# Seven quarter products for eight in the weighting of the values: an attention and cluster-MLP kernel on one core

## The chip, the cores and the metric

The kernel runs on one core of a Trainium2 chip, as one launch. The metric is the device time of that launch in microseconds (us), the median of several runs. The engines that a core has are called as in the profile: PE (TensorE; PEld is its loading of weights), DVE (VectorE), ACT (ScalarE), POOL (GpSimd) and SP (SyncE, which here only starts DMAs). They run side by side, each takes its own instructions strictly in the order of the program, and semaphores tie them together.

## What is computed

The input is four images of 256 channels and 64 x 64 pixels, f32 throughout. Two layers follow each other. The first is self-attention over the N = 4096 pixels of an image:

```python
q = jnp.einsum('oc,bcn->bno', wq, xf) + bq           # 32 channels
k = jnp.einsum('oc,bcn->bon', wk, xf) + bk[None, :, None]
attn = jax.nn.softmax(jnp.einsum('bnd,bdm->bnm', q, k), axis=-1)
v = jnp.einsum('oc,bcn->bon', wv, xf) + bv[None, :, None]
out = jnp.einsum('bcn,bmn->bcm', v, attn).reshape(B, Cc, H, W)
return gamma[0] * out + x
```

The second is a block with a clustering of the pixels and an MLP, each behind a group norm and with a residual:

```python
y = x + ls1 * cluster(group_norm(x, ...), f_w, f_b, v_w, v_b, proj_w, proj_b, alpha, beta)
hdn = conv1x1(jax.nn.gelu(conv1x1(group_norm(y, ...), mlp_w1, mlp_b1)), mlp_w2, mlp_b2)
y = y + ls2 * hdn
z = relu(batch_norm(y * dw_w, ...))
z = relu(batch_norm(conv1x1(z, pw_w), ...))
```

The change is in the product of v with the exponentials, the last einsum of the attention; the weights of the MLP and of the cluster are only stored elsewhere.

## The kernel before

**Stages.** The images are worked on one after the other. For each there are three stages: `weighting` (the attention), `cluster`, and `mlp`, which also computes the first scores of the next image. `alone` makes what the first image needs before its weighting. The program is written under `tc.manual_schedule()`: each engine executes what concerns it in the order in which the Python code issues it, and that order, made by hand, is all the schedule there is.

**Units and blocks.** The scores of an image are a 4096 x 4096 matrix. It is cut into `NBLK` = 8 blocks of 512 queries, a block into `GRP` = 8 units (steps) of 512 keys, so an image has 64 units. A unit's tile `s` in SBUF is 128 keys x 4 quarters x 512 queries. It goes through these functions:

- `score(u)` (L316): four products of 32 rows into two PSUM tiles of the pool `ps_s`, which has two such tiles. ACT copies both to `s` (L351, L356), DVE folds both into the running maximum `top` (L355, L358; L353 in the first unit of a block). Scores are made `LEAD` = 9 units ahead, by `due(u, quarter)`, which looks into the table `at`; in most units this happens ahead of the unit's first quarter.
- `across` and `spread`: the maximum over the keys is turned by PE (L369), reduced by DVE (L371), put on a diagonal (L373) and spread over all partitions by a product with ones (L383); the result `mb` stays in PSUM, in a tile of the pool `ps_m`, which has two. `across` runs ahead of the last quarter of unit 6 of the block before, `spread` right after the score of unit 7.
- `exps(u)`: DVE subtracts `mb` from each half of `s` (L395), ACT takes the exponential (L398), both in place; POOL adds the halves to the sum `acc` (L400, L403). It is issued one unit ahead.
- `weigh(u, av, quarter)` (L408): for each of four quarters, two products of 128 x 128 values with 512 columns of `s` are added to the two accumulators `av` in PSUM, one for each half of the channels. The accumulators have one buffer each, so the next block's first products wait until they are read.
- at the end of a block `gather` adds the two halves of `acc` (POOL, L420) and `clear` takes `av` out of PSUM, times gamma, one half by ACT (L424) and one by DVE (L425). During the next block follow `total` (L429), `inverse` (L435), `add` (POOL: times the inverse, L439, and onto the image, L444), `seen` and `pooled` (statistics, L448 and L453).

Each f32 product of PE appears as two MATMUL and two LDWEIGHTS instructions in the profile.

**Weights.** `w1_s`, `w2_s` and `mix` (the weights of the cluster's projections with room for 32 more columns) are loaded or made once at the start and stay. In `derived`, POOL turns two quarters of `w1_s` into the sums that the MLP needs, because `mlp` itself makes its hidden layer with seven quarter products of 256 columns in place of eight (L1126).

**What hides what.** `fill` takes products of the next image (or, in the last image, those of a block of the image before, `late_block`) and puts them where the chain of the group norm and the cluster leaves PE idle.

## Time and profile before

| what | value |
|---|---|
| median of three runs | 3478.5 us (3478.35 to 3481.72) |
| the profiled execution | 3478.09 us, of which its span 3476.0 us |
| mean granted clock of TensorE | 0.997 |
| PE busy | 3421.1 us, 98% of the span |
| DVE busy | 2046.2 us, 59% |
| ACT busy | 1683.9 us, 48% |
| POOL busy | 1489.2 us, 43% |

The span is the time from the first to the last instruction of one execution. Busy times count instructions under way, so an engine at 98% can still have a slower or a faster way to do the same. Of the groups of instructions (line, engine, operation, tile written <- tiles read, shape, count | busy us, mean ns | idle us before, and what ended it), these belong to the work around the change:

```profile
L408 PE MATMUL av<-s,v 128*128 128x512 f32 x4096 | 1826.5, 597 | 0.6 <-ACT s L398 0.6
L403 POOL TENSOR_TENSOR acc<-acc,s 128x1024 f32<-128x1024 f32 x448 | 1057.5, 2361 | 466.1 <-ACT s L398 446.7
L398 ACT ACTIVATE s<-s 128x1024 f32<-128x1024 f32 x512 | 538.7, 1057 | 462.8 <-DVE s L395 429.4
L395 DVE TENSOR_TENSOR s<-s,mb 128x1024 f32<-128x1024 f32 x512 | 595.2, 1207 | 6.5 <-PE mb L383 6.5
L355 DVE TENSOR_TENSOR top<-sc,top 128x1024 f32<-128x1024 f32 x196 | 239.9, 1224 | 388.0 <-PE sc L333 388.0
L333 PE MATMUL sc<-q,k 32*128 32x512 f32 x2048 | 294.0, 640 | 1.4 <-DMA q<-q 1.4
```

[...]

### The profile page before, as it was taken

Reading aid. Unit: us, or ns where it says so; the run is one execution under the profiler, and the core shown is the slowest. Engines: PE = TensorE matmul, PEld = TensorE weight load, DVE = VectorE, ACT = ScalarE, POOL = GpSimd, SP = SyncE. Lnnn points to the kernel's source line nnn. Section 1 sums busy time; section 2 is a strip of 40 time slices with the busy share of each in tenths; the row PEclk is TensorE's granted clock in tenths of the full one; section 3 lists DMA queues with packets and bytes.
Section 4 is the critical chain, followed back from the end, with each engine's and each line's share of the span. In section 5 each row is a group of like instructions: output and inputs, shape, how many; then the busy total and the mean of one; then the engine's idle time right before and its main releaser. Section 6 shows DMA issues by size and latency. Waiting matters only on the chain.

```text
span 3476.0 us, 31760 instructions
## 1 busy us (share of the span) xinstructions
PE 3421.1 (98%) x11760; PEld 1694.3 (49%) x11760; DVE 2046.2 (59%) x2912; ACT 1683.9 (48%) x2157; POOL 1489.2 (43%) x799
## 2 busy tenths in 40 slices
PE   8999999999999999999999999999999999999999
PEld 4444445655444444565544444466554444445565
DVE  4666664645566666464556666646446666664543
ACT  5545553444554554344455555434445554544444
POOL 2656665211265665521126566552104665672200
PEclk9999999999999999999999999999999999999999
DMA  2000001000000000100000000000000000000000
GB/s 91 7 4 3 7 0 49 7 19 13 20 5 4 3 7 12 37 7 19 19 16 4 3 5 5 19 30 7 19 19 10 4 7 3 4 0 1 13 19 25
DMA packets 25260, 47.16 MB, mean 14 GB/s; under 512 B 6704, under 2 KB 8592, under 8 KB 25104
## 3 DMA queue, kind: packets, MB, share of 16 engines
q1 hardware_dynamic: 20240, 38.29, 3.2%
q10 hardware_dynamic: 4608, 6.30, 0.8%
q8 instruction: 93, 1.52, 0.2%
q0 software_dynamic: 256, 0.52, 0.1%
q14 instruction: 63, 0.52, 0.0%
HBM read 19.93 MB, written 16.78 MB: 11 GB/s over the span
## 4 chain that ended last, share of the span: by engine, by line
PE 94%; DVE 3%; ACT 1%; DMA 0%; issue 0%; SPq 0%; POOL 0%; ACTq 0%; DVEq 0%
PE av L408 52%; PE mo L1133 12%; PE sc L333 8%; PE hu L1126 4%; PE pw L1102 3%; PE hp L1126 3%; PE hq L1126 3%; PE vp L285 2%; PE fv L790 2%; PE mb L383 1%; PE den L429 1%; PE op L911 1%; PE qp L304 0%; PE kp L262 0%; PE tt L369 0%
## 5 line engine op out<-in xcount | busy, mean ns | idle before, releaser
L408 PE MATMUL av<-s,v 128*128 128x512 f32 x4096 | 1826.5, 597 | 0.6 <-ACT s L398 0.6
L408 PEld LDWEIGHTS av<-s,v 128*128 128x128 f32 x4096 | 758.9, 190 | 1024.6 <-issue 1015.1
L403 POOL TENSOR_TENSOR acc<-acc,s 128x1024 f32<-128x1024 f32 x448 | 1057.5, 2361 | 466.1 <-ACT s L398 446.7
L398 ACT ACTIVATE s<-s 128x1024 f32<-128x1024 f32 x512 | 538.7, 1057 | 462.8 <-DVE s L395 429.4
L395 DVE TENSOR_TENSOR s<-s,mb 128x1024 f32<-128x1024 f32 x512 | 595.2, 1207 | 6.5 <-PE mb L383 6.5
L1133 PE MATMUL mo<-hs,w_s 128*128 128x512 f32 x992 | 508.4, 596 | 3.8 <-ACT hs L1155 1.6
L355 DVE TENSOR_TENSOR top<-sc,top 128x1024 f32<-128x1024 f32 x196 | 239.9, 1224 | 388.0 <-PE sc L333 388.0
L1155 ACT ACTIVATE hs<-hs,pv_s 128x256 f32<-128x256 f32 x496 | 251.3, 508 | 360.9 <-DVE hs L1162 350.1
L351 ACT COPY s<-sc 128x1024 f32<-128x1024 f32 x224 | 226.1, 1009 | 350.9 <-PE sc L333 350.9
L1162 DVE TENSOR_TENSOR hs<-hu,hs 128x256 f32<-128x256 f32 x372 | 157.8, 424 | 355.0 <-ACT hs L1165 205.5
L1088 POOL TENSOR_TENSOR xn<-xn 128x256 f32<-128x256 f32 x27 | 23.8, 881 | 681.7 <-DVE xn L1075 433.4
L333 PE MATMUL sc<-q,k 32*128 32x512 f32 x2048 | 294.0, 640 | 1.4 <-DMA q<-q 1.4
L400 POOL TENSOR_TENSOR acc<-s 128x1024 f32<-128x1024 f32 x32 | 75.1, 2347 | 476.9 <-ACT s L398 476.9
L358 DVE TENSOR_TENSOR top<-sc,top 128x1024 f32<-128x1024 f32 x196 | 240.1, 1225 | 47.5 <-ACT s L351 30.9
L356 ACT COPY s<-sc 128x1024 f32<-128x1024 f32 x224 | 226.9, 1013 | 76.0 <-DVE top L355 39.8
L1162 DVE TENSOR_TENSOR hs<-hq,hs 128x256 f32<-128x256 f32 x372 | 146.4, 421 | 107.5 <-PE hq L1126 103.3
L1133 PEld LDWEIGHTS mo<-hs,w_s 128*128 128x128 f32 x992 | 186.9, 190 | 42.7 <-ACT hs L1165 7.3
L333 PEld LDWEIGHTS sc<-q,k 32*128 32x128 f32 x2048 | 81.0, 182 | 192.5 <-issue 106.6
L1126 PE MATMUL hp<-xn,w_s 128*128 128x256 f32 x496 | 150.6, 385 | 2.7 <-DVE xn L1075 2.7
L1126 PEld LDWEIGHTS hp<-xn,w_s 128*128 128x128 f32 x496 | 92.4, 190 | 73.0 <-issue 62.4
L285 PE MATMUL vp<-wv_s,x 128*128 128x256 f32 x512 | 123.4, 387 | 0.2 <-ACT v L293 0.2
L1102 PE MATMUL pw<-xn,wpw_s 128*128 128x512 f32 x248 | 112.0, 594 | 3.4 <-ACT xn L1196 2.2
(215 smaller groups left out, 2823.0 us busy)
## 6 DMA issues: line engine op xcount, KB each, us to landing
x<-in_x SPq DMA_DIRECT2D x32, 512.0 KB, 4.6
out<-xn SPq DMA_DIRECT2D x62, 256.0 KB, 2.1
q<-q ACTq DMA_DIRECT2D x96, 64.0 KB, 2.0
w_s<-in_w SPq DMA_DIRECT2D x2, 1024.0 KB, 8.9
q<-q SPq DMA_DIRECT2D x24, 64.0 KB, 2.0
q<-q POOLq DMA_DIRECT2D x8, 64.0 KB, 6.4
out<-xl SPq DMA_DIRECT2D x2, 256.0 KB, 2.0
wv_s<-in_wv SPq DMA_DIRECT2D x1, 256.0 KB, 7.1
```

The source lines that it names most:

```text
L333: nc.tensor.matmul(halves[r // 2][:, r % 2, :], k_s[rows, g, :], q_s[rows, :], start=True, stop=True)
L355: nc.vector.tensor_tensor(top, halves[1], top, ALU.max)
L356: nc.scalar.copy(s[:, 2:4, :], halves[1])
L358: nc.vector.tensor_tensor(top, halves[0], top, ALU.max)
L395: nc.vector.tensor_tensor(sh, sh, mxs[nb].unsqueeze(1).to_broadcast([P, 2, NB]), ALU.subtract)
L398: nc.scalar.activation(sh, sh, AF.Exp)
L403: nc.gpsimd.tensor_tensor(acc, acc, s[:, 2 * h : 2 * h + 2], ALU.add)
L408: nc.tensor.matmul(av[c], own["v"][:, RG * g + quarter, c * P : (c + 1) * P], slots[u][:, quarter, :], start=(g == 0 and quarter == 0), st ...
L1126: nc.tensor.matmul(out, w[:, j * P : (j + 1) * P], x, start=True, stop=True)
L1133: yield nc.tensor.matmul(acc[c], w2_s[:, jj, c * P : (c + 1) * P], hs[:, i], start=(j == 0 and i == 0), stop=(j == HID // P // 2 - 1 and i ...
L1155: nc.scalar.activation(dst, src, act, bias=bias)
L1162: nc.vector.tensor_tensor(dst, ps, term, ALU.add)
```

## The change

In the units 2 to 6 of each block but an image's first (`SEVEN`), the product of v with the exponentials is no longer made quarter by quarter. A pair of the unit's value quarters gives a 2 x 2 matrix of blocks A (two row blocks: 128 channels each; two column blocks: 128 keys each), and the exponentials give B (two rows: the same keys; two columns: 256 queries each). Seven products of sums of these blocks replace the eight of blocks (Winograd's form). Each is issued for two pairs (i = 0, 1), with 256 columns.

- The sums of v are made once an image, in its first block, by DVE (`value_sums`), in place or in the memory of the MLP's weights, which are not needed then.
- The sums of the exponentials are made in each unit: two by DVE one unit ahead (`ready`), two by POOL in the unit itself, behind the product that still reads the old value (`by_seven`). The last two products read what POOL makes.
- Three of the products go to accumulators of their own (`pms`, both tiles of `ps_m`), and `combined` adds these up at unit 7, into `t`; `clear` then adds `av` to `t`, both halves by DVE.
- The sum `acc` over the keys, for the softmax, is taken from the sums made, where there are some.
- As `ps_m` is taken, the turned and the spread maximum use a tile of `ps_s`, and ACT copies the spread one to SBUF (`dg`), from where DVE's subtraction reads it.
- `spread` and the `exps` behind it are issued after the second quarter of unit 7; the score of unit 7 ahead of its last quarter, that of unit 0 ahead of its third, that of unit 1 ahead of its second.
- `add` is cut into two halves, at units 3 and 5; statistics come later.
- v is scaled by gamma when it is taken out of PSUM, so `clear` doesn't.
- `w1`, `w2` and `mix` are loaded for each image at the end of its weighting, and POOL's two sums of w1 made then.

The diff, cut:

```diff
+    own_w = {}
+    def load_mix(b):
+        own_w["mix"] = swap.tile([P, KC, 2, 2 * ED + 32], F32, tag="mix", name=f"mix_{b}")
+        for f in range(2):
+            nc.sync.dma_start(
+                out=own_w["mix"][:, :, f, 16 : 16 + 2 * ED],
+                in_=wfv.rearrange("(k p) m -> p k m", p=P),
+            )
...
+    def load_mlp(b):
+        w1_s = own_w["w1"] = swap.tile([P, KC, HID], F32, tag="w1", name=f"w1_{b}")
+        w2_s = own_w["w2"] = swap.tile([P, HID // P, C], F32, tag="w2", name=f"w2_{b}")
+        nc.sync.dma_start(out=w1_s, in_=w1.rearrange("(k p) m -> p k m", p=P))
+        nc.sync.dma_start(out=w2_s, in_=w2.rearrange("(k p) m -> p k m", p=P))
...
+        nc.gpsimd.tensor_tensor(w_cd, w_cd, w_d, ALU.add)
+        nc.gpsimd.tensor_scalar(w_d, w_d, -1.0, None, ALU.mult)
...
         def spread(nb, dg):
+            dg = dg.rearrange("p j n -> p (j n)")
+            if nb:
+                mb = ps_s.tile([P, 2, NB], F32, tag="s", name=f"mb_{b}_{nb}")[:, 0]
+            else:
+                mb = ps_m.tile([P, NB], F32, tag="m", name=f"mb_{b}_{nb}")
+            nc.tensor.matmul(mb, ones, dg, start=True, stop=True)
+            if nb:
+                nc.scalar.copy(dg, mb)
+            mxs[nb] = dg if nb else mb
...
+        def plain(u):
...
+            if g == 0:
+                nc.gpsimd.tensor_tensor(acc[:, 0], s[:, 0], s[:, 1], ALU.add)
+            for r in range(2 if g == 0 else 0, RG):
+                nc.gpsimd.tensor_tensor(acc[:, 0], acc[:, 0], s[:, r], ALU.add)
...
+        def ready(u):
+            b11, b12, b21, b22 = pairs(u)
+            nc.vector.tensor_tensor(u3_of(u), b12, b22, ALU.add)
+            nc.vector.tensor_tensor(b12, b12, b11, ALU.subtract)
...
+            product(av[0], 0, a12, b21)
+            product(pm[0], 0, a11, b11, start=one)
+            nc.gpsimd.tensor_tensor(b11, b11, u3, ALU.subtract)
+            nc.gpsimd.tensor_tensor(b21, b21, b11, ALU.add)
+            product(av[0], 1, w3, b22)
+            product(pm[1], 0, w7, u3, start=one)
+            product(pm[1], 1, s1, b12, stop=end)
+            acc = accs[nb][:, 1].rearrange("p (x n) -> p x n", x=2)
+            for x, t in enumerate((u3, b21)):
+                if one:
+                    nc.gpsimd.tensor_tensor(acc[:, x], t[:, 0], t[:, 1], ALU.add)
+                else:
+                    for i in range(2):
+                        nc.gpsimd.tensor_tensor(acc[:, x], acc[:, x], t[:, i], ALU.add)
+            between()
+            product(pm[0], 1, s2, b11, stop=end)
+            product(av[1], 0, a22, b21)
...
+            nc.scalar.copy(c11, p1)
+            nc.vector.tensor_tensor(c21, p6, c11, ALU.add)
+            nc.vector.tensor_tensor(c12, p5, c21, ALU.add)
+            nc.vector.tensor_tensor(c21, p7, c21, ALU.add)
+            nc.vector.tensor_tensor(c22, p5, c21, ALU.add)
...
         def clear(nb, av):
...
+            for c in range(KC):
+                nc.vector.tensor_tensor(ts[nb][:, c], av[c], ts[nb][:, c], ALU.add)
...
-        at = {(u, 0): u + LEAD for u in range(units - LEAD)}
+        place = {7: 3, 0: 2, 1: 1}
+        at = {(u, place.get(u % GRP, 0)): u + LEAD for u in range(units - LEAD)}
...
+                if u == units - 1:
+                    load_mix(b)
+                    load_mlp(b)
...
+                if seven(u):
+                    by_seven(u, av, beside)
+                    turn()
+                else:
                     weigh(u, av, 0)
                     due(u, 1)
                     weigh(u, av, 1)
+                    if g == GRP - 1 and more:
+                        spread(nb + 1, own["dg"])
+                        exps(u + 1)
+                        plain(u + 1)
+                    if nb and g == 0:
+                        total(nb - 1)
+                    due(u, 2)
+                    beside()
+                    weigh(u, av, 2)
+                    turn()
+                    due(u, 3)
+                    weigh(u, av, 3)
```

`beside` issues, for the unit ahead, `ready` or `plain`, and for the block before its inverse, its halves of `add` and its statistics. `turn` is `across` in unit 6.

## The prediction

> **What bounds the kernel now.** I read the page's chain of waits first, then the chain in one block of the attention, then the busy time of each engine over four such blocks, and last the timelines of DVE and POOL where they meet. The page's chain:

> ```profile
> PE 94%; DVE 3%; ACT 1%; DMA 0%; issue 0%; SPq 0%; POOL 0%; ACTq 0%; DVEq 0%
> PE av L408 52%; PE mo L1133 12%; PE sc L333 8%; PE hu L1126 4%; PE pw L1102 3%; PE hp L1126 3%; PE hq L1126 3%; PE vp L285 2%; PE fv L790 2%; PE mb L383 1%; PE den L429 1%; PE op L911 1%; PE qp L304 0%; PE kp L262 0%; PE tt L369 0%
> ```

> TensorE sets the end, and over half of that is the weighting of the values (L408). The chain inside a block has no hole:

> ```profile
> 1040.60 5.35 PE av L408 x12
> 1045.95 0.44 PE tt L369 x4
> 1046.39 1.72 PE av L408 x4
> 1048.11 1.07 PE sc L333 x8
> 1049.18 1.05 PE mb L383 x2
> 1050.23 6.87 PE av L408 x16
> 1057.10 1.07 PE sc L333 x8
> 1058.17 3.63 PE av L408 x8
> 1061.80 0.86 PE den L429 x2
> ```

> A logical f32 product is two instructions here: 8 of them are "x16" in 6.87 us, 0.429 us an instruction of 512 columns. With the changes of shape around the score (0.1 us each) a step is 7.07 + 1.07 us. A block of eight steps takes 67.1 us (69.1 with the next queries, L304), and the other engines have this to do in it:

> ```profile
> core 0: us, PE busy (x) PEld busy (x) DVE busy (x) ACT busy (x) POOL busy (x), PEclk, DMA share, GB/s
> 1049.18:1118.27 69.09, 69.09 (x217) 27.73 (x217) 44.75 (x42) 35.18 (x36) 41.63 (x18) 1.00 0.02 5
> 1118.27:1185.40 67.13, 67.13 (x200) 27.23 (x200) 44.76 (x42) 35.13 (x35) 41.64 (x18) 1.00 0.02 4
> ```

> DVE 44.8 and POOL 41.6 of 67.1 us: a third is free on each, if they can run side by side. The next lines are where they do not. DVE's fold (L363) reads two tiles of SBUF, POOL's L420 too:

> ```profile
> 1043.54 1.59 POOL L420 TENSOR_TENSOR rden<-acc 128x512 f32<-128x512 f32 x1
> ...
> 1043.29 0.72 DVE L363 TENSOR_TENSOR top<-top 128x512 f32<-128x512 f32 x1
> ...
> 975.10 1.28 POOL L420 TENSOR_TENSOR rden<-acc 128x512 f32<-128x512 f32 x1
> ...
> 976.05 0.89 DVE L363 TENSOR_TENSOR top<-top 128x512 f32<-128x512 f32 x1
> ```

> Where POOL came 0.25 us after the fold, it took 1.59 us instead of 1.26 to 1.28: it waited 0.31 of the 0.47 us that the fold still had. Where the fold came while POOL had 0.33 us left, it took 0.89 instead of 0.69. So one waits for the other's end less 0.14 us. Against DVE's L395 (one input in PSUM) POOL's L403 keeps its 2.36 us, and L395 its 1.21.

> [...]

> **The change, part by part.**

> *Products.* A changed step has 7 products of 2 pairs at 256 columns: 28 instructions in place of 16 of 512. Consecutive instructions of L1126 (256 columns) start 0.216 us apart, so 28 x 0.216 = 6.05 us for 6.87: 0.82 us gained. Steps: 5 x 7 blocks (not the first) x 4 images = 140, so **-115 us** if nothing waits. A changed step is then 6.05 + 1.07 + about 0.1 = 7.2 us, a block 63.1. The weight load is 0.19 us, under 0.216, as in L1126.

> *Block boundary.* The maximum's spread (L383) went from the start of step 7 to behind its second quarter, and the score of step 7 from the start to before its last quarter. DVE now clears both halves of av (before: ACT and DVE one each). What is queued ahead of that clearing, counted from the start of step 7: products to 3.43, mb to 4.29, then in turn ACT's copy of mb 0.6, DVE's two subtractions 2 x 1.21, the second exp 1.06, ACT's copy of the score (in ACT's queue behind that exp) 1.01, DVE's maximum of the score (L353) 1.22, the first clear 0.69, some 0.1 for each of seven hand-overs: 4.29 + 7.0 + 0.7 = 12.0 us. TensorE is done with the step at 3.43 + 0.86 + 1.72 + 1.07 + 1.72 = 8.8 and needs the cleared accumulator for its next product. It waits 3.1 us where before it had none. Six boundaries of an image have such a score (the seventh has no later unit): 24 x 3.1 = **+74 us**.

> *POOL and DVE.* Subtractions: mb is copied to SBUF, so 16 of them a block now have two SBUF inputs. "ready" adds 10 DVE instructions of 512 elements (0.685 each, L346), all from SBUF. POOL: in a changed step two of 512 (L936, L1059: 1.27) and four of 256 (L1090: 0.724; two in the first); 5.4 us where L403 took 4.72. add: four of 512, 5.1 us in steps 3 and 5. The new wait is TensorE's own: the last two products read b11 and b21, which POOL makes in the same step after product 2. Without a clash they come in time: 2.6 us of POOL against products 3 to 5 and 6, 3.46 us.
> Now the stretch from POOL's first b11 (step 2) to its last b21 (step 6). POOL: 5 x 2.54 + 14 x 0.724 + 5.1 = 27.9 us. DVE in that time: 8 subtractions 9.7, 8 "ready" 5.5. They exclude each other; take 16 x 2 x 0.14 = 4.5 off for hand-overs, add 1.1 for POOL's gaps of 0.075 between its own. 27.9 + 15.2 - 4.5 + 1.1 = 39.7 us. TensorE would be there after 4 x 7.2 + 3.46 = 32.3. It waits 7.4 us a block. Last block of an image: no scores, 28.1 us of TensorE, so 11.6. 24 x 7.4 + 4 x 11.6 = **+224 us**. The bounds: over a whole block the sum of both engines is 46.8 + 27.6 (with fold and dg) - 7.8 + 1.3 = 67.9 us against 63.1, so 4.8 a block or 135 us if every lag could be worked off in steps 7, 0 and 1; and 0 if the clashes fell into POOL's idle time. Above: DVE has 54 us of work in a block and strict order; its waits delay its maxima, which hold the two score buffers, so up to 10 a block, 280 us. I take the middle sum, as the wait is within a step and can't be worked off later.

> *Rest.* Sums of the values (20 DVE instructions of 256 in the first block, 8 us an image): DVE has 20 us idle there, 0. "combined", 4 x 0.42 and one ACT copy at the start of step 7: before the spread, 0 (1.7 a block if DVE is late, within the bound above). v scaled on ACT at 0.69 for 0.585: ACT is half idle, 0. tt and mb in the score's buffers: free in those quarters, 0. At an image's end the clear goes ahead of the reciprocal: 2 x 0.69, **+5 us** for four. The weights: SP gets four DMAs at the last step, behind the x loads; nothing but outputs stands behind them. W1 landed in 8.9 us at the start; POOL's two of 1.27 wait for it, with "begin" behind them. Only in the last image is W1 read at once, by the fill after the last step: 0 to 8, taken as **+3**. The start drops 2 MB behind the x loads: 0.

> Sum: -115 + 74 + 224 + 5 + 3 = +191 on 3478 (the profiled execution: span 3476.0, 3478.1 with 2.1 around it; the median of the runs, 3478.5, is the same): **3670 us**.

> **Rivals.**
> 1. Faster: DVE's clashes fall into POOL's 37% idle time, so that TensorE never waits for b11 or b21. For: POOL needs only 5.4 of 7.2 us, and TensorE's wait at the boundary lets both catch up. Against: 67.9 us of both in 63.1. Time: 3478 - 115 + 74 + 8 = 3445. It decides where clashes cost POOL under 1.3 us a changed step (7.2 less 5.4 of work and 0.45 of gaps), of the 3.8 us that DVE's four instructions hold. With the boundary hidden too, by work that I put in the wrong order, 3371.
> 2. Lags are worked off in the plain steps, only the sum binds: 4.8 us a block, of which the boundary's 3.1 is a part: 3478 - 115 + 135 + 8 = 3506.
> 3. Likeliest, both waits stand: 3670, its own range 3550 (5 a block with the boundary half hidden) to 3740 (10 a block).

> **Chances.** Likeliest 0.70, rival 2 0.10, rival 1 0.15 and 0.05 with the boundary hidden. A measurement of this kernel tells about 0.2% (7 us) from no change. Faster 0.18, within 0.2% 0.04 (between rivals 1 and 2), slower 0.78. The range 3435 to 3740 leaves out half of the faster cases below and the worst stalls above.

> **What will show it.** Right: DVE's L395 line well over 1.21 us in mean (1.6 or more); POOL's 512-element additions over 1.27; the chain of waits going through POOL and DVE, over 5%; TensorE waiting for POOL at the last two products, and for DVE at each block's first product; blocks of 70 to 76 us. Wrong: blocks near 63 us, L395 at 1.2, or POOL idle before each b11 for want of TensorE's product 2.

## The result, and the profile after

The kernel with the change takes 3827.6 us (median of four runs, 3826.2 to 3829.0), the kernel before, on the same chip, 3478.9: a ratio of 1.100 with the interval [1.0981, 1.1019], 349 us more. The forecast was 3670 us. Its sign holds, its size doesn't: the time lies above the range (3435 to 3740).

The page of the kernel after; first the two lines of its chain of waits, then groups (busy us, mean ns of one, idle us before and what ended it):

```profile
PE 49%; DVE 32%; POOL 7%; ACT 6%; issue 6%; DMA 0%; SPq 0%; POOLq 0%; ACTq 0%; DVEq 0%
DVE s L417 13%; PE av L545 11%; PE mo L1305 11%; DVE top L374 5%; PE hu L1298 4%; ACT s L367 4%; DVE s L486 3%; PE pw L1274 3%; PE hp L1298 3%; PE hq L1298 3%; PE vp L299 3%; DVE u L485 2%; PE sc L349 2%; DVE rden L585 2%; PE av L503 2%
...
L545 PE MATMUL av<-s,v 128*128 128x512 f32 x1856 | 895.9, 631 | 107.3 <-DVE t L575 84.2
...
L417 DVE TENSOR_TENSOR s<-s,dg 128x1024 f32<-128x1024 f32 x448 | 678.6, 1554 | 28.4 <-ACT dg L409 28.0
...
L439 POOL TENSOR_TENSOR acc<-acc,s 128x512 f32<-128x512 f32 x280 | 383.6, 1370 | 80.2 <-ACT s L420 62.2
L513 POOL TENSOR_TENSOR s<-s,u 128x512 f32<-128x512 f32 x140 | 196.0, 1400 | 435.2 <-PE pm L503 196.3
...
L374 DVE TENSOR_TENSOR top<-sc,top 128x1024 f32<-128x1024 f32 x196 | 240.1, 1225 | 133.3 <-ACT s L367 129.0
...
L503 PE MATMUL pm<-s,vs_w 128*128 128x256 f32 x560 | 167.6, 426 | 149.2 <-POOL s L513 147.7
```

In the chain TensorE fell from 94% to 49%, and DVE (32%) and POOL (7%) came in. The subtraction, now L417 with both inputs in SBUF, takes 1554 ns in mean where it took 1207. POOL's 512-element sums take 1370 and 1400 ns; alone, in the kernel before, sums of this size took 1270 (L936, L1059). TensorE waits 147.7 us for the first sum of POOL (L513) and 84.2 us for DVE's clearing of the accumulators (L575).

One block of the attention, as busy time by engine:

```profile
core 0: us, PE busy (x) PEld busy (x) DVE busy (x) ACT busy (x) POOL busy (x), PEclk, DMA share, GB/s
1314.00:1392.30 78.30, 67.97 (x261) 39.71 (x260) 61.78 (x58) 34.34 (x36) 57.57 (x46) 0.96 0.02 4
```

A block took 67.1 us and takes 78.3. DVE is busy for 61.8 us of it (44.8 before), POOL for 57.6 (41.6), and TensorE for 68.0 us, although it has less to do than before. The timeline of TensorE in that block (start, duration, line, tiles, count, and in brackets the wait ahead of the group and what ended it):

```profile
1317.73 1.98 PE L545 MATMUL av<-s,v 128*128 128x512 f32 x4
1323.78 5.37 PE L545 MATMUL av<-s,v 128*128 128x512 f32 x8 [4.07 <-DVE t L575]
...
1365.42 1.13 PE L503 MATMUL pm<-s,vs_w 128*128 128x256 f32 x4 [2.37 <-POOL s L513]
...
1384.51 1.17 PE L503 MATMUL pm<-s,vs_w 128*128 128x256 f32 x4 [2.83 <-POOL s L513]
1386.17 2.07 PE L503 MATMUL av<-s,v 128*128 128x256 f32 x4 [0.50 <-POOL s L514]
...
1388.89 3.60 PE L545 MATMUL av<-s,v 128*128 128x512 f32 x8
```

Two things are to be seen. First, the waits: 4.07 us for the clearing at the start of the block, 2.37 and 2.83 us for POOL's first sum. Second, what comes after them: the eight products at 1323.78 take 5.37 us, where the eight at 1388.89 take 3.60. The trace's clock records show TensorE at half rate for 3.41 us from 1324.03 on, and again from 1385.47 on, where the four products at 1386.17 take 2.07 us in place of 1.13 (1365.42).

Why does POOL come late at 1365.42? Its own timeline ahead of that, and then two lines of DVE's:

```profile
1357.74 1.97 POOL L524 TENSOR_TENSOR acc<-acc,s 128x256 f32<-128x256 f32 x2
1359.67 2.26 POOL L590 TENSOR_TENSOR t<-t,rden 128x512 f32<-128x512 f32 x1
1362.01 2.14 POOL L593 TENSOR_TENSOR x<-x,t 128x512 f32<-128x512 f32 x1
1364.10 1.27 POOL L513 TENSOR_TENSOR s<-s,u 128x512 f32<-128x512 f32 x1
```

```profile
1351.07 2.29 DVE L417 TENSOR_TENSOR s<-s,dg 128x1024 f32<-128x1024 f32 x2
...
1359.11 3.90 DVE L417 TENSOR_TENSOR s<-s,dg 128x1024 f32<-128x1024 f32 x2
```

The sum at 1364.10 takes 1.27 us, as long as POOL's sums of this size take alone, but it starts late. Two halves of `add` are ahead of it (L590, L593), and each took over 2.1 us (1.27 alone) because DVE's two subtractions were under way from 1359.11 on. These in turn took 3.90 us, and 2.29 in the step before (1351.07), where POOL read nothing at that time.

This step is no exception. Of the 57 waits for L513 in the whole trace, 28 are in step 4 (74.7 us) and 28 in step 6 (72.4 us), the two steps behind a half of `add`; the steps 3 and 5 have none. So the wait doesn't grow from step to step. It comes where `add` stands ahead of POOL's sums.

### The profile page after: what moved, and what is told of

Its sections match the earlier page's. It is cut to its first block, busy times and chain, and to the rows that moved or that the text cites. A ratio compares the mean times of both kernels' runs of the same rounds, so it can differ in the third digit from the quotient of the medians.

```text
span 3824.4 us, 36351 instructions
## 1 busy us (share of the span) xinstructions
PE 3475.4 (91%) x13440; PEld 2071.1 (54%) x13440; DVE 2612.5 (68%) x3415; ACT 1676.4 (44%) x2189; POOL 1945.5 (51%) x1559
## 4 chain that ended last, share of the span: by engine, by line
PE 49%; DVE 32%; POOL 7%; ACT 6%; issue 6%; DMA 0%; SPq 0%; POOLq 0%; ACTq 0%; DVEq 0%
DVE s L417 13%; PE av L545 11%; PE mo L1305 11%; DVE top L374 5%; PE hu L1298 4%; ACT s L367 4%; DVE s L486 3%; PE pw L1274 3%; PE hp L1298 3%; PE hq L1298 3%; PE vp L299 3%; DVE u L485 2%; PE sc L349 2%; DVE rden L585 2%; PE av L503 2%
## 5 line engine op out<-in xcount | busy, mean ns | idle before, releaser
L545 PE MATMUL av<-s,v 128*128 128x512 f32 x1856 | 895.9, 631 | 107.3 <-DVE t L575 84.2
L420 ACT ACTIVATE s<-s 128x1024 f32<-128x1024 f32 x512 | 540.4, 1057 | 904.7 <-DVE s L417 894.7
L417 DVE TENSOR_TENSOR s<-s,dg 128x1024 f32<-128x1024 f32 x448 | 678.6, 1554 | 28.4 <-ACT dg L409 28.0
L545 PEld LDWEIGHTS av<-s,v 128*128 128x128 f32 x1856 | 362.2, 202 | 607.7 <-issue 570.8
L1305 PE MATMUL mo<-hs,w 128*128 128x512 f32 x992 | 507.6, 595 | 3.8 <-ACT hs L1327 1.6
L439 POOL TENSOR_TENSOR acc<-acc,s 128x512 f32<-128x512 f32 x280 | 383.6, 1370 | 80.2 <-ACT s L420 62.2
L513 POOL TENSOR_TENSOR s<-s,u 128x512 f32<-128x512 f32 x140 | 196.0, 1400 | 435.2 <-PE pm L503 196.3
L503 PE MATMUL av<-s,v 128*128 128x256 f32 x1120 | 344.5, 438 | 20.8 <-POOL s L514 20.3
L374 DVE TENSOR_TENSOR top<-sc,top 128x1024 f32<-128x1024 f32 x196 | 240.1, 1225 | 133.3 <-ACT s L367 129.0
L503 PEld LDWEIGHTS av<-s,v 128*128 128x128 f32 x1120 | 220.9, 211 | 171.2 <-issue 93.7
L503 PE MATMUL pm<-s,vs_w 128*128 128x256 f32 x560 | 167.6, 426 | 149.2 <-POOL s L513 147.7
L349 PE MATMUL sc<-q,k 32*128 32x512 f32 x2048 | 294.6, 642 | 0.0
L503 PE MATMUL pm<-s,v 128*128 128x256 f32 x1120 | 288.3, 380 | 0.0
L372 ACT COPY s<-sc 128x1024 f32<-128x1024 f32 x224 | 227.4, 1015 | 56.2 <-DVE top L369 45.9
L367 ACT COPY s<-sc 128x1024 f32<-128x1024 f32 x224 | 223.5, 998 | 36.4 <-PE sc L349 36.4
L524 POOL TENSOR_TENSOR acc<-acc,s 128x256 f32<-128x256 f32 x224 | 233.9, 1044 | 8.8
L503 PEld LDWEIGHTS pm<-s,v 128*128 128x128 f32 x1120 | 213.5, 191 | 29.4
```

Of the source, the lines that this page charges most:

```text
L349: nc.tensor.matmul(halves[r // 2][:, r % 2, :], k_s[rows, g, :], q_s[rows, :], start=True, stop=True)
L367: nc.scalar.copy(s[:, 0:2, :], halves[0])
L374: nc.vector.tensor_tensor(top, halves[0], top, ALU.max)
L417: nc.vector.tensor_tensor(sh, sh, mxs[nb].unsqueeze(1).to_broadcast([P, 2, NB]), ALU.subtract)
L420: nc.scalar.activation(sh, sh, AF.Exp)
L439: nc.gpsimd.tensor_tensor(acc[:, 0], acc[:, 0], s[:, r], ALU.add)
```

## The experiments

The questions: is it the exclusion of DVE's subtractions and POOL, or only that DVE and POOL have more work? Is the wait at the block's start a cost of its own? What does the halved clock cost? And what is left when these are gone? The base is the kernel after, except for the first run. Each run stands with what the theories expected of it. Line numbers shift by a few in edited kernels.

### The exclusion by itself: the kernel before, with the maximum in SBUF

```diff
+            dg = dg.rearrange("p j n -> p (j n)")
             nc.tensor.matmul(mxs[nb], ones, dg, start=True, stop=True)
+            if nb:
+                nc.scalar.copy(dg, mxs[nb])
+                mxs[nb] = dg
```

> The kernel before, with one part of the change alone: the spread maximum is copied from PSUM to SBUF by ACT, and DVE's subtraction reads it there. Theory A (DVE with two SBUF inputs and POOL exclude each other): L395 grows from 1.21 us to 1.5 or more in mean and L403 from 2.36 to 2.6 or more, while the time changes little (0 to +20 us), since here TensorE never waits for POOL within a step and both engines have a third of the block free. Theory B (DVE is slow in the changed kernel for its amount of work and its order alone): L395 stays at 1.21, L403 at 2.36, time the same.

3488.6 us, ratio 1.0026 [1.0017, 1.0036]. The groups of its trace:

```profile
L405 POOL TENSOR_TENSOR acc<-acc,s 128x1024 f32<-128x1024 f32 x448 | 1132.6, 2528 | 386.7 <-ACT s L400 365.8
L397 DVE TENSOR_TENSOR s<-s,dg 128x1024 f32<-128x1024 f32 x448 | 834.7, 1905 | 45.0 <-ACT dg L386 45.0
...
L363 DVE TENSOR_TENSOR top<-top 128x512 f32<-128x512 f32 x32 | 58.2, 1818 | 1.1
```

The subtraction (L397) went from 1207 to 1905 ns, POOL's sum of the exponentials (L405) from 2361 to 2528, the fold (L363) from 738 to 1818. Nothing differs but the place of one input and the copy that puts it there (one a block), so the exclusion is real and large: 448 x 0.70 = 313 us of DVE's time. Yet the kernel lost only 10 us. In this kernel TensorE needs nothing that POOL makes within the step, and DVE is a step ahead. Here longer DVE instructions cost only where somebody waited for them.

### Without the subtraction's second input

```diff
-                nc.vector.tensor_tensor(
-                    sh, sh, mxs[nb].unsqueeze(1).to_broadcast([P, 2, NB]), ALU.subtract
-                )
+                if nb:
+                    dummy = small.tile([P, 2], F32, tag="dummy", name=f"du_{b}_{u}_{h}")
+                    nc.vector.tensor_reduce(dummy, sh, AX.X, ALU.max)
+                else:
+                    nc.vector.tensor_tensor(
+                        sh, sh, mxs[nb].unsqueeze(1).to_broadcast([P, 2, NB]), ALU.subtract
+                    )
```

> The changed kernel, in which each subtraction of the maximum with two SBUF inputs is replaced by a DVE reduction of the same 1024 elements into two numbers that nobody uses: one SBUF input, about the same 1.21 us. The maximum isn't subtracted in these blocks. Theory A: the exclusion is what makes POOL late, so TensorE's waits for b11 and b21 (149 and 21 us) fall to a third or less, and the time falls by 150 to 250 us. Theory B: DVE has the same amount of work in the same order, so the time falls by less than 50 us.

3523.8 us, 304 less than after; ratio to before 1.0128 [1.0111, 1.0145]. Groups, then two lines of the waits (total us, times, longest):

```profile
L419 DVE TENSOR_REDUCE du<-s 128x2 f32<-128x1024 f32 x448 | 516.3, 1192 | 0.0
...
L517 POOL TENSOR_TENSOR s<-s,u 128x512 f32<-128x512 f32 x140 | 179.6, 1283 | 403.9 <-PE pm L507 185.5 <-DVE top L371 169.7 <-ACT s L424 27.0
```

```profile
PE pm L507 <- POOL s L517: 37.0, 56, 1.7
...
PE av L549 <- DVE t L579: 32.6, 20, 1.6
```

The reduction (L419) takes 1192 ns, as the subtraction did in the kernel before, and DVE has as many instructions as in the kernel after. So it is not the amount of DVE's work; it is the exclusion. One thing more goes with the edit: DVE no longer waits for the copy of the maximum (28.0 us in the kernel after, L417 for L409). What that alone brings, no run shows. In the trace's clock records and waits, TensorE's wait for POOL goes (147.7 to 37.0 us), so does most of that for the clearing (84.2 to 32.6) and of the half-rate time (306 to 46 us; the mean clock is 0.993). TensorE's idle time fell by 181 us, and half of the half-rate time saved at work is (282 - 40) / 2 = 121 us: together 302 of the 304. The clock came along, so it was more than expected.

### The wait at the start of a block

The score of step 7 is put behind the clearing of the accumulators, so that DVE's maximum isn't ahead of it:

```diff
-        at = {(u, place.get(u % GRP, 0)): u + LEAD for u in range(units - LEAD)}
+        at = {
+            (u + 1, 0) if u % GRP == 7 else (u, place.get(u % GRP, 0)): u + LEAD
+            for u in range(units - LEAD)
+        }
```

> The changed kernel, with the score of step 7 issued at the start of the next step 0, behind the clearing of the accumulators, and nothing else moved. If the clearing waits for that score's maximum in DVE's queue, the waits of L545 for L575 (84 us, 24 times) go, and with them the halved clock that follows each: 24 x (4.2 + 1.7) = -140 us. Rival: the wait at the boundary is where DVE and POOL catch up, so it comes back as waits for POOL in steps 2 to 6, and less than 50 us is left.

3831.2 us, ratio 1.1008 [1.0981, 1.1035]: no gain. TensorE's waits:

```profile
PE pm L503 <- POOL s L513: 142.4, 57, 4.9
...
PE sc L349 <- ACT s L367: 30.7, 21, 2.0
...
PE av L545 <- DVE t L575: 26.5, 24, 2.1
...
PE sc L349 <- ACT s L372: 20.7, 21, 1.2
```

The wait for the clearing fell from 84.2 to 26.5 us, as meant, but nearly as much came up in front of the scores, which now wait for ACT's copies (30.7 and 20.7 us; neither group waited before the edit). In all, TensorE's idle time fell by 19 us and its half-rate time rose a little (at work from 282 to 289 us).

The rival's reading, that the block's start is where DVE and POOL catch up and that they stay late if it is closed, fits this, but isn't shown. The edit makes a wait of its own: step 0 now has two scores, the moved one at its start and its own ahead of the third quarter, and it is the second that waits for its buffers. The run with both edits, below, shows this wait without the exclusion too.

### Useless work in the wait

Eight products of 256 columns into a tile that nobody reads, ahead of each block's first product (but an image's first block):

```diff
+                    if g == 0 and nb:
+                        idle = ps_m.tile([P, NB], F32, tag="m", name=f"idle_{b}_{nb}")
+                        for _ in range(8):
+                            nc.tensor.matmul(
+                                idle[:, :C], ones, wpw_s[:, 0, :], start=True, stop=True
+                            )
                     weigh(u, av, 0)
```

> The changed kernel, with eight products (256 columns, 3.5 us) that nobody uses ahead of each block's first product, so that TensorE works where it waited for the clearing. Theory C (part of the loss is TensorE's clock, halved for 3.4 us after each wait of some 4 us): the halved stretch after the boundary goes, 24 x 1.7 = -40 us, though work was added. Rival (the halved clock costs nothing, because something else is late there): the time is the same, or longer by what the added work delays.

3779.8 us, 48 less than after; ratio 1.0865 [1.0848, 1.0881]. The line of its core:

```profile
core 0: 3777.1 us, clock 0.975
```

Its mean clock is 0.975 (0.960 after). TensorE at work stood at half rate for 177 us in place of 282; half of the difference, 52 us, is what the products get back. The work added (28 blocks x 16 instructions x 0.216 = 97 us) fills waits: TensorE's idle time fell by 90 us. A kernel that does more takes less: the clock is a cost of its own.

### The two together, and POOL's sums

The reduction in place of the subtraction and the moved score:

> Both edits together: the reduction in place of the subtraction (so the maximum isn't subtracted), and the score of step 7 behind the clearing. With the first alone a block took 67.5 us with 1.6 us of waiting for the clearing in it; with the second alone nothing was gained. If the second gained nothing because the clash of DVE and POOL set the block's length, it gains now: 24 x 1.6 = -40 us against the first alone, about 3485, near the kernel before. If the order of DVE's work sets the length without the clash too, the time stays at 3524.

3529.9 us, ratio 1.0145 [1.0128, 1.0162]; with the reduction alone it was 1.0128 [1.0111, 1.0145]. So the moved score brings nothing without the exclusion either. The waits for the clearing are gone (32.6 us, and 8.2 for ACT's half `t`), but the second score of step 0 waits for ACT's copy, 24 times and 17.1 us, and that costs more than it shows (below): start to start, the scores take 321 us where they took 277. The edit pays for the wait that it closes with one of its own.

The kernel after, without POOL's sums of the exponentials in the steps 3 to 6:

```diff
-                else:
-                    for i in range(2):
-                        nc.gpsimd.tensor_tensor(acc[:, x], acc[:, x], t[:, i], ALU.add)
```

> The changed kernel without POOL's additions to the softmax sums in the steps 3 to 6 (16 of 256 elements a block, 11.6 us of POOL), so the sums are incomplete; the subtraction with two SBUF inputs stays. Theory A [...] nearly all waits for POOL go and the time falls by 250 us or more, to 3480 to 3580. Theory D (POOL's two sums of each step are late because DVE's subtractions lie just ahead of them, whatever POOL does else): less than 120 us is gained.

3687.1 us, 140 less than after; ratio 1.0591 [1.0576, 1.0607]. This lies between what the theories gave. Theory A's figure comes from the prediction's sum of DVE's and POOL's times in a block, an estimate: 67.9 us, some 57 without these sums, under TensorE's 63. POOL's load matters, but 448 sums less of it bring under half of what one input of the subtraction does. The waits for L513 are nearly gone (5.3 us), but TensorE now waits 65.3 us for DVE's fold (`tt` for `top`, L379; 15.2 in the kernel after) and 38.6 for L514 (20.3).

Three steps of a block with seven products in place of five (`SEVEN = (2, 4, 6)`):

> The changed kernel with seven products in the steps 2, 4 and 6 of a block, in place of 2 to 6. The gain of the products would be 3/5 of 115, 69 us. POOL's work between two of these steps falls to a plain step's, so what is late can be made up in steps 3 and 5: [...] waits are few and mostly those at the boundary (about 90 us with their halved clock): 3480 to 3560. If each such step waits as it does now (some 1.2 us and its clock), 3650.

3709.7 us, ratio 1.0661 [1.0645, 1.0677]: 231 us lost with three steps, 349 with five, so 77 and 70 us for each changed step of a block. The expectation missed: by the same sum it counted some 65 us of DVE and POOL in a block against TensorE's 64.7, an estimate. In a block of 74.2 us POOL is busy for 59.0 and DVE for 61.4 (57.6 and 61.8 of 78.3 with five), and TensorE waits 4.3 us for the clearing at the start of each. Two changed steps less take no work from POOL, since a plain step has its own sums there. TensorE's waits for POOL's two sums fell (168 to 75.5 us, per changed step from 1.2 to 0.9), so a part of the lag is made up in the plain steps. But the wait for the clearing rose (84.2 to 96.0 us), TensorE at work still stood at half rate for 157 us, and the products gain less. The halves of `add` stand in just these plain steps, 3 and 5.

All three edits together (no second input, the score moved, fewer sums):

> All three edits: no subtraction of the maximum with two SBUF inputs (a reduction in its place), the score of step 7 behind the clearing, no additions to the softmax sums in steps 3 to 6. If the products' own gain is the 115 us that I took, and nothing else in the change costs TensorE anything but 10 to 20 us at the ends of the images, the time is 3375 to 3400. If it stays above 3440, something else in the change costs TensorE that I haven't named.

3510.9 us, ratio 1.0094 [1.0079, 1.0109]. Even so it is slower than the kernel before. DVE's timeline over one step:

```profile
1382.87 2.27 DVE L419 TENSOR_REDUCE du<-s 128x2 f32<-128x1024 f32 x2
1385.07 1.21 DVE L371 TENSOR_TENSOR top<-sc,top 128x1024 f32<-128x1024 f32 x1
1387.17 1.23 DVE L374 TENSOR_TENSOR top<-sc,top 128x1024 f32<-128x1024 f32 x1 [0.90 <-ACT s L367]
1388.31 0.68 DVE L489 TENSOR_TENSOR u<-s 128x512 f32<-128x512 f32 x1
1389.03 0.69 DVE L490 TENSOR_TENSOR s<-s 128x512 f32<-128x512 f32 x1
1389.64 0.95 DVE L586 RECIPROCAL rden<-rden 128x128 f32<-128x128 f32 x1
1390.50 2.28 DVE L419 TENSOR_REDUCE du<-s 128x2 f32<-128x1024 f32 x2
```

From one reduction to the next it takes 1390.50 - 1382.87 = 7.63 us, with no clash in it. DVE's instructions fill 6.7 us, and 0.90 is a wait inside: the second maximum (L374) waits for ACT's copy (L367). TensorE's changed step needs 7.31 us (below). So DVE falls behind in each of them, and at the block's end TensorE waits for its fold (`tt` for `top`, L379): 28 times, 56.7 us. It also waits 33.1 us for ACT's copy in front of the second half of a score (L349 for L372, 48 times).

### Another order on DVE

In the changed steps the maxima of the scores go ahead of the subtractions, and `inverse` ahead of `ready`:

```diff
-                if g + 1 < GRP:
-                    exps(u + 1)
-                else:
-                    gather(nb)
+                if g + 1 == GRP:
+                    gather(nb)
+                elif not seven(u):
+                    exps(u + 1)
...
                 due(u, 0)
+                if seven(u):
+                    exps(u + 1)
...
                 def beside():
+                    if nb and 0 < g < 5:
+                        inverse(nb - 1, (g - 1,))
...
-                        elif g < 5:
-                            inverse(nb - 1, (g - 1,))
```

> The changed kernel with DVE's order changed in the seven-product steps alone: the score's two maxima ahead of the subtractions for the next step, the inverse ahead of ready. Theory E (DVE's turn of a step is a ring: subtractions, second exp, ACT's copy of the score behind it, second maximum, ready, inverse: 2.2 + 1.0 + 1.0 + 1.2 + 1.4 + 0.9 = 7.7 us, over TensorE's 7.2, before any clash): the 0.9 us of waiting inside it goes, 5 x 0.9 us a block at most, so up to 28 x 4.5 = 126 us, and with the clash still there some 40 to 130 us is gained. If only the clash counts: within 30 us of 3827.

3897.9 us, ratio 1.1201 [1.1179, 1.1222], 70 more than after. The groups:

```profile
L417 DVE TENSOR_TENSOR s<-s,dg 128x1024 f32<-128x1024 f32 x448 | 803.3, 1832 | 36.5 <-ACT dg L409 36.5
...
L503 PE MATMUL av<-s,v 128*128 128x256 f32 x1120 | 364.6, 453 | 91.0 <-POOL s L514 75.0 <-ACT s L420 15.6
...
L514 POOL TENSOR_TENSOR s<-s 128x512 f32<-128x512 f32 x140 | 268.2, 1916 | 11.0
```

The subtractions now fall onto the time in which POOL makes its two sums: L417 takes 1832 ns and L514 1916, and TensorE waits 75.0 us for the latter (20.3 after). In both orders the exclusion hits something that TensorE waits for; a third order wasn't tried.

With the moved score in addition:

> The same order of DVE, and the score of step 7 behind the clearing. Nothing is left out. If the ring was why the second edit alone gained nothing, it gains now, 40 us or more against the order alone. If the clash is why, nothing.

3901.4 us, ratio 1.1212 [1.1192, 1.1233]: the same.

The new order, the reduction in place of the subtraction, and the moved score:

> The same, with the reduction in place of the subtraction (the maximum isn't subtracted). It was 3530 in the old order. Theory E: the ring no longer binds, a block falls from 67.5 us to 64 or 65, and the time by 28 x 2.5 to 28 x 3.5 = 70 to 100 us, to 3430 to 3460, under the kernel before. If it stays above 3510, the ring isn't what was left.

3567.4 us, ratio 1.0248 [1.0231, 1.0264], 38 more than with the old order. The reductions come later in the step now, and with them ACT's exponentials: TensorE waits 29.4 us for these in the plain steps, where it waited 0.7 with the old order.

And with fewer sums as well:

> All edits: the order, the score behind the clearing, no subtraction, no additions to the softmax sums in steps 3 to 6. It was 3511 in the old order. Theory E and the products' own gain of 115 us: a block near 63.5, the time 3370 to 3410. Above 3470 the gain of the products is smaller than I counted or still eaten by something unnamed.

3465.4 us, ratio 0.9953 [0.9938, 0.9969], 45 less than with the old order (the wait for the fold went from 56.7 to 15.2 us) and the first time under that of the kernel before. But two parts of the computation are missing in it, so it is a bound and not a version. TensorE's timeline:

```profile
1325.51 1.13 PE L349 MATMUL sc<-q,k 32*128 32x512 f32 x4
1327.35 1.13 PE L349 MATMUL sc<-q,k 32*128 32x512 f32 x4 [0.71 <-ACT s L372]
1328.41 5.42 PE L546 MATMUL av<-s,v 128*128 128x512 f32 x12
1333.76 1.14 PE L349 MATMUL sc<-q,k 32*128 32x512 f32 x8
1334.83 5.42 PE L546 MATMUL av<-s,v 128*128 128x512 f32 x12
...
1348.56 1.13 PE L507 MATMUL av<-s,v 128*128 128x256 f32 x4
...
1355.87 1.13 PE L507 MATMUL av<-s,v 128*128 128x256 f32 x4
...
1363.18 1.13 PE L507 MATMUL av<-s,v 128*128 128x256 f32 x4
...
1378.07 3.70 PE L546 MATMUL av<-s,v 128*128 128x512 f32 x8 [0.83 <-ACT s L424]
```

The changed steps start 7.31 us apart (1348.56, 1355.87, 1363.18), without a hole. That is what the scheme gives if nothing waits: 8.14 - 7.31 = 0.83 us a step. Two waits are left in a block, 0.83 us at step 7 and 0.71 inside the second score of step 0. The latter costs more than 0.71. The eight instructions of a score start four at a time: in the kernel after, four of L349 within 20 ns of each other and the next four 0.53 us later. The eight take 1.07 us (1333.76 to 1334.83), and four alone take as long (1.13), so the score that is cut in two by the wait takes 2.90 us (1325.51 to 1328.41), 1.83 more. A block takes 66.0 us in place of 67.1.

No version that computes everything was faster than the kernel before. Not tried: the maximum kept in PSUM, which would take the second SBUF input away without leaving anything out; the two tiles that held it carry three of the seven products. Nor was `add` moved out of the steps 3 and 5, though nearly all waits for POOL's first sum lie behind it.

## Why the prediction was right in sign and too low

**Products (-115).** Right: 140 x 0.83 = 116 us, measured where nothing waits.

**Block boundary (+74).** As a wait it is right: 24 times, 84.2 us, 3.5 us each (the prediction's own 12.0 - 8.8 is 3.2 and not 3.1). Whether it is a term of its own, to be added to the clash, stays open: moving the score takes 58 us of it away and the time doesn't change, but that edit brings a wait of its own. The prediction called this wait something that "lets both catch up" in its first rival, and added it to the clash all the same.

**POOL and DVE (+224).** The mechanism is right: DVE's subtraction at 1.6 us or more was asked for and 1.55 came, POOL's additions over 1.27 us, the chain through POOL and DVE over 5% (39%), the waits at the last two products. The picture of a lag that grows from step 2 to step 6 isn't what the trace shows: the waits for the first sum lie in the steps 4 and 6, behind `add`. As a wait it was too large: 147.7 + 20.3 = 168 us. As a cause it was too small: without the second input of the subtraction 304 us go, above the upper bound of 280, since most of the boundary's wait and of the halved clock go with it.

**Rest (+8).** Not tested by itself. The first block of an image, which I put at nothing, has a new wait for ACT's copy (`t`, L571): four times, 22.4 us in all. The wait for the fold (`tt` for `top`, L379) is new too: four times, 15.2 us.

**The step that failed: the sum has no term for the clock.** Every product in it is taken at full rate. The waits were forecast well in their sum, 74 + 224 + 8 = 306 us: between the matmuls the trace shows 335 us of idle time and 41 in the kernel before, 294 more. That this fits is partly luck, as POOL's term was 56 us too large and some 40 us of waits were forecast nowhere. But TensorE stood at half rate for 306 us (23 before), and for 282 of these (18.5) it was at work. Half of the difference is lost: (282 - 18.5) / 2 = 132 us. The sum then is -116 + 294 + 132 = 310 of the 348 us. The run with useless work shows that this term isn't just another name for the waits.

Of the trace's 77 half-rate stretches 63 are 3.41 us long, 13 are twice that, and the last is 3.88. A wait of 3.1 us, as forecast for the block's start, is shorter than any of them, but waits shorter still have one in them or just behind: 36 of the 57 between 2 and 3 us (last section).

The 38 us that remain lie in the products of the weighting, beside their waits. Counted from start to start, without the idle time and half of the half-rate time, these products take 1801 us in the kernel before (L408) and 1725 in the kernel after (L545, L503), 76 less and not 116; all others together differ by 2 us. In the last run above, where next to nothing waits in the changed steps, they take 1689 us, 112 less. A part of it is how the holes are counted: an end of a matmul is modelled some 0.17 us past the start of the next one (four products of L545 show 1.98 us at 1317.73, and behind the four at 1314.85 the next starts after 1.81; in the kernel before, those of L408 show 597 ns in mean and start 429 ns apart), so each hole is that much longer than it looks. There are 254 holes in the trace after and 89 in that before; 165 x 0.17 = 28 us, an estimate.

**Rivals.** The first rival needed POOL's loss under 1.3 us a changed step; the two sums of `add` alone lost 1.9 us in the step shown above. The second, that lags are worked off in the plain steps, falls with the 168 us of waits within the steps; the run of three steps shows that plain steps work off only a part.

## What to carry to other kernels

A scheme that trades TensorE's products for sums is worth its 0.83 us a step only if the sums have free engines to run on. Here DVE and POOL weren't two engines where DVE's subtraction had both inputs in SBUF: beside POOL's sums it took 1905 ns in place of 1207 in the kernel before, and without its second input the changed kernel takes 304 us less. Before an operand is moved from PSUM to SBUF to free its tile, count the instructions that read it. Where a forecast contains waits of TensorE of 2 us or more, add what its clock loses afterwards, here up to 1.7 us for each, and so with 68 of the 89 such waits in the kernel after. And where closing a wait doesn't move the time, see where the idle time went before concluding that the wait was free: the edit may have opened another.
